# Turning two layers' inputs with VectorE and DRAM instead of TensorE, and a seam listed anew

## The chip, the cores and the metric

One core of a Trainium2 chip runs the whole kernel in one launch, in float32. The metric is the time of one execution on the device in microseconds (us). Four engines compute: TensorE (PE), VectorE (DVE), ScalarE (ACT) and GpSimd (POOL). SyncE (SP) issues nearly all DMA transfers.

## The reference

The input x is (2, 2048, 256): 4096 tokens of 256 features. Four layers follow, each a layer norm, a function and a residual sum:

```python
x = x + attention_a(layernorm(x))   # softmax attention, 16 heads, 4 key heads
x = x + ffn(layernorm(x))           # "rotations", first time
x = x + attention_b(layernorm(x))   # causal linear attention
x = x + ffn(layernorm(x))           # "rotations", second time

def ffn(x):                         # four-layer coupling net, per token: 256-256-128-64-1
    gf = global_net(mean over tokens of x)
    for _ in range(3):
        tf = coupling_net(x)
        x = x + (0.1 + range * (0.7 * gf + 0.3 * tf - 0.5) * 2) * twist(x)

def attention_b(x):                 # 16 heads of 16
    q, k, v = rope(silu(x @ Wq)), rope(silu(x @ Wk)), x @ Wv
    out = tril(q @ k.T) @ v         # no softmax
    out = out * sigmoid(x @ Wg1 @ Wg2)
    return layernorm(out) @ Wo
```

## The kernel before

`xs` holds all tokens in SBUF with tokens on partitions (32 tiles of 128x256); layer norms read it so. Projections need the features on partitions, so each normalised tile must be transposed ("turned"). `zq` is the buffer of all tokens turned, 128 x 2 x 4096, in which the rotations work. The work is cut into eight blocks of 512 tokens (`BLK`), four for each of the two sequences.

`attention_a` runs to about 1500 us, and the first rotations, `rotations(0, ...)`, to about 1690. Then come eight `Block` objects of the linear attention, one loop turn each, to about 1950, and the second rotations, `rotations(1, ...)`, which begin while block 7 is still at work and end at 2102. `in_order(begin)` ties the instructions of PE, DVE, ACT and POOL from line 738 on to the order in which the program lists them; SP's queue keeps its own listed order too. The listing by hand is thus the schedule: an instruction that waits holds up everything that stands behind it on its engine. PSUM gives seven banks in turn (`bank`) and one for the running sums (`ps_state`); a bank's next writer waits for its last reader.

What a turn of the main loop lists, for block x, with y the block after, `after` the one after that, `before` the one ahead:

- `energies(t)`, t = 0 to 3 (L1127, L1133): PE multiplies keys and queries of 128 tokens into four banks, DVE masks them into `en`. `learn(t)` (L1171, L1177) updates the state, `output(t)` (L1144, L1153, L1158) multiplies state and `en` into a bank `bpo`, and DVE gates that into `og`.
- Between them stand y's projections: `query` and `key` (PE L975 pq, pk; ACT silu L1028; POOL products with cosine and sine; DVE shuffles L1035), `rotate` (DVE adds L1047), `narrow` and `gates` (L1069, L1085), `values` (L984 pv), `keys_by_tokens` (PE transposes L996 pt), `halve` and `ready` (ACT L1103 qeo, L1113).
- For the block after that: `look` (DVE statistics of the layer norm, POOL power L111), `norm` (ACT scales into a tile `zt`, L124; POOL adds to xs), and `turn`: `turn(z, bank, evacuate)` makes eight PE transposes of 128x128 into two banks (L131, `bztr`), which ACT copies to `z` (L1022).
- For the finished x: `project_out` (PE L984 pw, L996 pog; DVE statistics L106 to L110 and POOL L111), `add_out` (DVE L1193 into xs). For `before`, whose tokens are then ready for the next layer: `next_look`, `next_norm` (ACT L124 into a tile `zt` of the pool `late`, which has one buffer for it) and `next_turn`: eight PE transposes (L131, `ztr`), which ACT copies to `zq` (L1209) with a sum over the tokens into `sums1`, that the global net needs.

The seam is the change from the first rotations to block 0. `fourth(11, amid)` is the last step of the rotations; for k of 8 and more it is `back`, in which PE transposes blocks of zq back (`turn_back`) and DVE adds them to xs (L879, L912), for two blocks (e) in two halves (h) each. `amid`, called once between the two blocks, lists rotate and key of block 0. After it stand `zero.rotate()` and so on.

The second rotations' tail: when block 7's loop turn is over, its `next_look`, `next_norm` and `next_turn` are listed among `first`, `second`, `third`, `fourth` (PE L817 q1f, L827 q2f, L839 q3f, L852 q4f; ACT a1f, a2f, a3f, cf; DVE and POOL update zq). `context(1)`, resumed by `next(front1)`, is the global net of the second sequence (DVE gmf L781 and L782, PE p1f L786).

Stores to DRAM are already part of `attention_a`: there the key maxima of 128x32 are turned by DVE (L403) and placed through DRAM (dm, L407, L412).

Of the kernel before, what the change touches and what calls it, by code (L numbers as in the profile page):

```python
# [9 lines left out]
F32 = mybir.dt.float32  # L10
F32R = mybir.dt.float32r
AF = mybir.ActivationFunctionType
# [4 lines left out]
P = 128  # L17
B, N, D = 2, 2048, 256
T = B * N
BLK = 512  # L20
NB = T // BLK
# [46 lines left out]
def tile_hybrid(ctx: ExitStack, tc: tile.TileContext, x: bass.AP, consts: bass.AP, wa_d: bass.AP, wf_d: bass.AP, wb_d: bass.AP, out: bass.AP):  # L68
    nc = tc.nc
# [8 lines left out]
    zq = keep.tile([P, 2, T], F32, name="zq")  # L78

    own = ctx.enter_context(tc.tile_pool(name="own", bufs=1))  # L80
    dram = ctx.enter_context(tc.tile_pool(name="a_dram", bufs=2, space=bass.MemoryType.DRAM))
# [12 lines left out]
    def blk(t, j):  # L94
        return t[:, :, j * BLK : (j + 1) * BLK]
# [628 lines left out]
    def behind(tail):  # L724
# [3 lines left out]
        work = ctx.enter_context(tc.tile_pool(name="work", bufs=1, reuse_waits="tile"))  # L728
# [7 lines left out]
        def take(tag, shape, name):  # L736
            if tag == "kt2":
                return work.tile(shape, F32, tag="kt", name=name)
            if tag in ("og", "kt", "swap"):
                return own.tile(shape, F32, tag=tag, name=name, bufs=2 if tag == "swap" else 1)  # L740
            return work.tile(shape, F32, tag=tag, name=name, bufs=rings.get(tag, 1))
# [31 lines left out]
        def rotations(n, part, store):  # L773
# [31 lines left out]
            def blocks(k):  # L805
                return 2 * (k % 4), 2 * (k % 4) + 1
# [59 lines left out]
            def turn_back(k, e, h):  # L866

                j = blocks(k)[e]
                z = blk(zq, j)
                tr = bank(f"trf{n}_{k}_{e}_{h}")  # L870
                for q in range(2):
                    at = slice((2 * h + q) * P, (2 * h + q + 1) * P)
                    for c in range(2):
                        to = q * D + (1 - c) * P
                        nc.tensor.transpose(tr[:, to : to + P], z[:, c, at], ident)
                tr = tr.rearrange("p (q s f) -> p q s f", q=2, s=2)
                half = tokens(j)[:, 2 * h : 2 * h + 2, :].rearrange("p q (s f) -> p q s f", s=2)
                for s in range(2):
                    nc.vector.tensor_tensor(half[:, :, s, :], half[:, :, s, :], tr[:, :, 1 - s, :], ALU.add)  # L879
                return half, tr  # L880
# [5 lines left out]
            def back(k, js, a3, between):  # L886


                q4 = bank(f"q4f{n}_{k}")
                for tile in range(4):  # L890
                    mm(
                        q4[:, 2 * tile : 2 * tile + 2], a3[:, tile * P : (tile + 1) * P], w4_pair,
                        start=True, stop=True,
                    )
                cs = take("small", [P, 3, 8], f"cf{n}_{k}")
                nc.scalar.activation(cs[:, 2, :], q4[:, 0:8], AF.Tanh, bias=hb4, scale=0.5)
                nc.vector.tensor_scalar(cs[:, 0, :], cs[:, 2, :], plain, plains[js[0] // BPB], ALU.mult, ALU.add)
                nc.vector.tensor_scalar(cs[:, 1, :], cs[:, 0, :], -1.0, None, ALU.mult)
                for e in range(2):
                    j = js[e]  # L900
                    if e == 1 and between:
                        between()
                    for h in range(2):
                        half, tr = turned.pop((k, e, h), None) or turn_back(k, e, h)
                        for q in range(2):
                            tile = 2 * h + q

                            x4, t4 = (
                                a.rearrange("p s (u f) -> p (s u) f", u=2) for a in (half[:, q, :, :], tr[:, q, :, :])
                            )  # L910
                            for m, quarters in enumerate((slice(0, 4, 3), slice(1, 3))):
                                nc.vector.scalar_tensor_tensor(  # L912
                                    x4[:, quarters, :], t4[:, quarters, :], cs[:, m, 2 * tile + e : 2 * tile + e + 1],
                                    x4[:, quarters, :], ALU.mult, ALU.add,
                                )
                        if store:
                            s0 = (j % BPB) * BLK + 2 * h * P
                            nc.sync.dma_start(
                                out[j // BPB, s0 : s0 + 2 * P, :].rearrange("(t p) d -> p t d", p=P),
                                tokens(j)[:, 2 * h : 2 * h + 2, :],  # L920
                            )
# [4 lines left out]
        sums1 = hold.tile([P, 2, NB], F32, name="sums1")  # L926
# [72 lines left out]
        class Block:  # L999
# [19 lines left out]
            def turn(self):  # L1019
                j = self.j  # L1020
                self.z = take("z", [P, 2, BLK], f"bz{j}")
                turn(self.zt, lambda c: bank(f"bztr{j}_{c}"), lambda c, tr: nc.scalar.copy(self.z[:, c, :], tr))  # L1022
# [21 lines left out]
            def rotate(self):  # L1044
# [2 lines left out]
                        nc.vector.tensor_tensor(r[:, m, :], r[:, m, :], ts[m], ALU.add)  # L1047
                self.turning = []

            def query(self):  # L1050
                self.q = self.rotated(wq, "qs", "rotq")

# [36 lines left out]

            def keys_by_tokens(self):  # L1090

                self.values(1)
                self.kt = take("kt2" if self.j % 2 else "kt", [P, 4, D], f"kt{self.j}")
                for h in range(2):
                    p = transposed(self.k, h, f"t{self.j}")
                    nc.scalar.copy(self.kt[:, 2 * h : 2 * h + 2, :].rearrange("p t d -> p (t d)"), p)
# [106 lines left out]
                scale(self.fzt, self.tile_of, *self.scales)  # L1203

            def next_turn(self):
                j = self.j
                turn(
                    self.fzt, lambda c: bank(f"ztr1_{j}_{c}"),
                    lambda c, tr: nc.scalar.activation(  # L1209
                        zq[:, c, j * BLK : (j + 1) * BLK], tr, AF.Copy, accum_out=sums1[:, c, j : j + 1]  # L1210
                    ),
                )


        blocks = [Block(j) for j in range(NB)]
# [21 lines left out]
        f = rotations(0, sums0, False)  # L1237
        context, first, second, third, fourth, _ = f
# [72 lines left out]
        zero, one = blocks[0], blocks[1]  # L1311
# [16 lines left out]
            zero.rotate()  # L1328
            zero.key()

        fourth(11, amid)
        zero.rotate()
        zero.narrow()
        zero.values(0)
        zero.gates()
        zero.halve(0)
        zero.keys_by_tokens()
        zero.ready(0)
        one.turn()

        f = rotations(1, sums1, True)
        context, first, second, third, fourth, turn_ahead = f
        front, front1 = context(0), context(1)
        for j, x in enumerate(blocks):
            before = blocks[j - 1] if j else None
            y = blocks[j + 1] if j + 1 < NB else None
            after = blocks[j + 2] if j + 2 < NB else None
            x.energies(0)
            if before:
                before.add_out(1)  # L1350
            if j == NB - 2:
                next(front)
            if y:
                y.query()
            else:
                first(0, 0)
            x.learn(0)
            x.output(0)
            x.energies(1)
            if j == NB - 2:  # L1360
                next(front)
            if before:
                before.next_look()
            if y:
                y.rotate()
                y.key()
            else:
                first(0, 1)
            x.learn(1)
            x.output(1)  # L1370
            if y:
                y.narrow()
            x.energies(2)
            if before:
                before.next_norm()
            if j == NB - 2:
                next(front)
            if y:
                y.gates()
                y.values(0)  # L1380
                y.rotate()
            else:
                first(1, 0)
            if after:
                after.look()
            x.learn(2)
            x.output(2)
            x.energies(3)
            if j == NB - 2:
                next(front)  # L1390
            if y:
                y.keys_by_tokens()
                y.ready(0)
            else:
                first(1, 1)
            if after:
                after.norm(work)
            x.project_out(0)
            x.learn(3)
            x.output(3)  # L1400
            if after:
                after.turn()
            if not y:
                second(0)
            x.add_out(0)
            x.project_out(1)
            if before:
                before.next_turn()
# [6 lines left out]
        fourth(0)  # L1415
        first(2, 1)
        third(1)
        x.next_turn()
        next(front1)
        second(2)  # L1420
# [134 lines left out]
```

## Time and profile before

| | |
|---|---|
| Time, median of 3 runs | 2103.09 us (2100.2 to 2106.34) |
| Profiled execution: its own time | 2103.77 us |
| Profiled execution: span, first to last instruction | 2102.0 us |
| Granted TensorE clock, mean | 0.995 |
| Busy PE, DVE, ACT, POOL | 99%, 81%, 68%, 17% |
| Transposes of PE at L131: bztr, ztr | 64 and 112, of which 64 ztr belong to the second rotations' input |

Times in a profile are those of one execution. An engine's row gives the start, the length, the line and operation, output and inputs, and the idle time before it with what ended it. Matmuls are pipelined, so PE's cost of a step is read from start to start. L12 is line 12 of the kernel before.

### The profile page before, as it was taken

Reading aid. Unit: us, or ns where it says so; the run is one execution under the profiler, and the core shown is the slowest. Engines: PE = TensorE matmul, PEld = TensorE weight load, DVE = VectorE, ACT = ScalarE, POOL = GpSimd, SP = SyncE. Lnnn points to the kernel's source line nnn. Section 1 sums busy time; section 2 is a strip of 40 time slices with the busy share of each in tenths; the row PEclk is TensorE's granted clock in tenths of the full one; section 3 lists DMA queues with packets and bytes.
Section 4 is the critical chain, followed back from the end, with each engine's and each line's share of the span. In section 5 each row is a group of like instructions: output and inputs, shape, how many; then the busy total and the mean of one; then the engine's idle time right before and its main releaser. Section 6 shows DMA issues by size and latency. Waiting matters only on the chain.

```text
span 2102.0 us, 38754 instructions
## 1 busy us (share of the span) xinstructions
PE 2082.3 (99%) x14158; PEld 1010.6 (48%) x14158; DVE 1698.0 (81%) x3241; ACT 1427.3 (68%) x2787; POOL 355.1 (17%) x352
## 2 busy tenths in 40 slices
PE   9999999999999999999999999999999999999998
PEld 4444444444444444444444444444444567776434
DVE  6999988998998999899899899988134678886336
ACT  4477777777777777777777777778864445554443
POOL 3100010000001000000000000000135455542451
PEclk9999999999999999999999999999999999999999
DMA  6511010111101011010110101100100000000002
GB/s 199 149 44 40 18 37 17 50 30 27 38 18 47 10 47 40 17 48 10 47 39 19 38 19 48 37 20 8 53 1 1 0 2 1 1 2 1 1 0 81
DMA packets 59696, 68.72 MB, mean 33 GB/s; under 512 B 24944, under 2 KB 34032, under 8 KB 59248
## 3 DMA queue, kind: packets, MB, share of 16 engines
q1 hardware_dynamic: 58592, 64.79, 11.6%
q8 instruction: 111, 1.82, 0.4%
q10 hardware_dynamic: 720, 0.92, 0.1%
q14 instruction: 81, 0.66, 0.1%
q0 software_dynamic: 192, 0.52, 0.1%
HBM read 35.78 MB, written 26.21 MB: 29 GB/s over the span
## 4 chain that ended last, share of the span: by engine, by line
PE 96%; DVE 2%; DMA 1%; ACT 1%; POOL 0%; issue 0%; SPq 0%; DVEq 0%; ACTq 0%
PE av L632 24%; PE s L376 23%; PE p L650 11%; PE q1f L817 8%; PE p L654 7%; PE q2f L827 4%; PE pe L1127 2%; PE bpo L1153 2%; PE pq L975 1%; PE po L499 1%; PE pw L984 1%; PE pv L984 1%; PE pq L336 1%; PE pk L975 1%; PE q3f L839 1%; PE q4f L852 1%
## 5 line engine op out<-in xcount | busy, mean ns | idle before, releaser
L380 DVE TENSOR_REDUCE mx<-s 128x1 f32<-128x512 f32 x2048 | 1272.8, 682 | 107.0 <-PE s L376 101.2
L658 ACT ACTIVATE e<-p 128x512 f32<-128x512 f32 x2048 | 1057.6, 603 | 308.6 <-PE p L654 301.7
L376 PE MATMUL s<-a_kP,qP 64*128 64x512 f32 x2048 | 706.7, 470 | 4.0 <-DVE mx L380 2.1
L654 PE MATMUL p<-a_m,a_pick 64*128 64x512 f32 x2048 | 580.4, 415 | 0.0
L376 PEld LDWEIGHTS s<-a_kP,qP 64*128 64x128 f32 x2048 | 283.5, 184 | 568.9 <-DVE mx L380 532.1
L632 PE MATMUL av<-e,a_v 128*32 128x512 f32 x4096 | 547.3, 605 | 0.1
L650 PE MATMUL p<-qP,a_kP 64*128 64x512 f32 x2048 | 522.1, 393 | 1.9 <-ACT e L658 1.9
L650 PEld LDWEIGHTS p<-qP,a_kP 64*128 64x128 f32 x2048 | 283.5, 186 | 61.4 <-issue 15.9
L654 PEld LDWEIGHTS p<-a_m,a_pick 64*128 64x128 f32 x2048 | 282.2, 184 | 27.2
L817 PE MATMUL q1f<-zq,wf 128*128 128x512 f32 x384 | 176.1, 601 | 0.0
L632 PEld LDWEIGHTS av<-e,a_v 128*32 128x32 f32 x4096 | 81.0, 108 | 129.1 <-issue 120.0
L398 POOL TENSOR_TENSOR mt<-nm,mt 128x16 f32<-128x16 f32 x31 | 6.9, 222 | 743.9 <-ACT mt L397 743.9
L818 ACT ACTIVATE a1f<-q1f,wf 128x512 f32<-128x512 f32 x96 | 65.8, 686 | 94.5 <-PE q1f L817 91.2
L817 PEld LDWEIGHTS q1f<-zq,wf 128*128 128x128 f32 x384 | 70.3, 190 | 96.9 <-issue 86.2
L1133 DVE TENSOR_TENSOR en<-pe,small 128x512 f32<-128x512 f32 x128 | 79.3, 681 | 14.2 <-PE pe L1127 14.2
L858 DVE TENSOR_SCALAR cf<-cf,f_beta,alphaf 128x512 f32<-128x512 f32 x32 | 32.7, 1022 | 67.7 <-ACT cf L857 67.7
L827 PE MATMUL q2f<-a1f,wf 128*128 128x512 f32 x192 | 87.0, 595 | 0.0
L237 POOL TENSOR_TENSOR ql<-zq,qh 128x512 f32<-128x512 f32 x15 | 19.2, 1283 | 364.2 <-ACT qh L234 364.2
L862 POOL TENSOR_TENSOR tf<-cf,zq 128x512 f32<-128x512 f32 x32 | 56.6, 1768 | 102.4 <-DVE cf L858 101.9
L829 ACT ACTIVATE a2f<-q2f,wf 128x512 f32<-128x512 f32 x48 | 32.6, 685 | 56.2 <-PE q2f L827 56.2
L864 POOL TENSOR_TENSOR zq<-zq,tf 128x512 f32<-128x512 f32 x32 | 56.8, 1775 | 2.5
L491 POOL TENSOR_TENSOR oc<-oc,sums 128x512 f32<-128x512 f32 x16 | 20.5, 1284 | 211.9 <-DMA sums<-dr 140.3
(210 smaller groups left out, 1634.9 us busy)
## 6 DMA issues: line engine op xcount, KB each, us to landing
qP<-dq SPq DMA_DIRECT2D x64, 256.0 KB
dq<-qh SPq DMA_DIRECT2D x62, 128.0 KB
dq<-ql SPq DMA_DIRECT2D x62, 128.0 KB
a_kP<-dk SPq DMA_DIRECT2D x16, 256.0 KB
oc<-avs SPq DMA_DIRECT2D x128, 32.0 KB
sums<-dr SPq DMA_DIRECT2D x128, 32.0 KB
out<-xs SPq DMA_DIRECT2D x16, 256.0 KB
xs<-in_x SPq DMA_DIRECT2D x7, 512.0 KB
```

The costliest lines, as they stand in the source:

```text
L376: mm(s, qP[r // 2][row, qi * P : (qi + 1) * P], kP[r // 2][row, k0 + kb * BLK : k0 + (kb + 1) * BLK], start=True, stop=True,)
L380: nc.vector.tensor_reduce(mx[:, r, qi : qi + 1, kb], s, AX.X, ALU.max)
L632: mm(av[32 * r : 32 * r + 32, :], vA[:, units[u][0] // BPB * KB + kb, 32 * r : 32 * r + 32], es[r], start=(kb == 0), stop=(kb == KB - 1),)
L650: mm(t[r], kP[r // 2][row, k0 : k0 + P], qP[r // 2][row, :], start=True, stop=False)
L654: mm(t[r], pick[row, :], mrow[r // 2][row, :], start=False, stop=True)
L658: nc.scalar.activation(es[r], t[r], AF.Exp, scale=1.0 / HD**0.5)
L817: mm(q1, w1[:, c, m * P : (m + 1) * P], z[:, c, :], start=(c == 0), stop=(c == 1))
L818: nc.scalar.activation(a1[:, m, :], q1, AF.Gelu, bias=b1[:, m : m + 1])
L827: mm(q2, w2[:, c, :], a1[:, c, :], start=(c == 0), stop=(c == 1))
L862: nc.gpsimd.tensor_tensor(t1, cs, z[:, 0, :], ALU.mult)
L864: nc.gpsimd.tensor_tensor(z[:, 1, :], z[:, 1, :], t1, ALU.subtract)
L1133: nc.vector.tensor_tensor(self.ens[t][w], pes[w].rearrange("p (h n) -> p h n", h=4), const("triu").unsqueeze(1).to_broadcast([P, 4, P]), A ...
```

## The change

1. The seam: `back` calls one of two functions before each half of its second block, `amid` before the first half and `zero.rotate` before the second. `zero.values(1)` and `one.turn()` move ahead of `zero.halve(0)` and `zero.keys_by_tokens()`.
2. Blocks 2 to 7 of the linear attention aren't turned by PE. `squares` lets DVE transpose each 128x256 tile of `zt` in place, in squares of 32x32. Four DMAs per tile write the squares to a DRAM tile at the places where they belong, each with 32 partitions x 8 pieces of 32 elements. `fetch` reads the DRAM tile into `z` with two DMAs of 128 x 2 KB. `look` moves up to behind `energies(0)`, `norm` to ahead of `learn(1)`; `squares((0, 1))` stands behind y's `rotate`, `squares((2, 3))` and `fetch` behind y's `ready(0)`. Blocks 0 and 1 are turned by PE as before.
3. `next_turn` does the same for blocks 0 to 6, with a DRAM tile `dz` and two fetches into `zq`; block 7 stays with PE. The sums over tokens come from `next_sum`, two ACT activations from zq to itself with an accumulator, two loop turns later (block 6's ahead of block 7's `next_turn`).
4. `values(1)` is called ahead of `keys_by_tokens` rather than in it, with the same order on PE.

```diff
@@ back
                 for e in range(2):
                     j = js[e]
-                    if e == 1 and between:
-                        between()
                     for h in range(2):
+                        if e == 1 and between:
+                            between[h]()
                         half, tr = turned.pop((k, e, h), None) or turn_back(k, e, h)
@@ Block
+            def squares(self, ts):
+                if 0 in ts:
+                    self.placed = dram.tile([D, BLK], F32, tag="db", name=f"db{self.j}")
+                at = self.placed.rearrange("(b f) (t a i) -> t a f b i", f=32, a=4, i=32)
+                for t in ts:
+                    nc.vector.transpose(self.zt[:, t, :], self.zt[:, t, :])
+                    for a in range(4):
+                        nc.sync.dma_start(
+                            at[t, a], self.zt[32 * a : 32 * a + 32, t, :].rearrange("f (b i) -> f b i", i=32)
+                        )
+
+            def fetch(self):
+                self.z = take("z", [P, 2, BLK], f"bz{self.j}")
+                for c in range(2):
+                    nc.sync.dma_start(self.z[:, c, :], self.placed[c * P : (c + 1) * P, :])
...
             def keys_by_tokens(self):
-                self.values(1)
...
             def next_turn(self):
                 j = self.j
+                if j + 1 < NB:
+                    to = dram.tile([D, BLK], F32, tag="dz", name=f"dz{j}")
+                    at = to.rearrange("(b f) (t a i) -> t a f b i", f=32, a=4, i=32)
+                    for t in range(4):
+                        nc.vector.transpose(self.fzt[:, t, :], self.fzt[:, t, :])
+                        for a in range(4):
+                            nc.sync.dma_start(
+                                at[t, a],
+                                self.fzt[32 * a : 32 * a + 32, t, :].rearrange("f (b i) -> f b i", i=32),
+                            )
+                    for c in range(2):
+                        nc.sync.dma_start(
+                            zq[:, c, j * BLK : (j + 1) * BLK], to[c * P : (c + 1) * P, :]
+                        )
+                    return
                 turn(
...
+            def next_sum(self):
+                for c in range(2):
+                    z = zq[:, c, self.j * BLK : (self.j + 1) * BLK]
+                    nc.scalar.activation(z, z, AF.Copy, accum_out=sums1[:, c, self.j : self.j + 1])
@@ seam
-        fourth(11, amid)
-        zero.rotate()
+        fourth(11, (amid, zero.rotate))
         zero.narrow()
         zero.values(0)
         zero.gates()
+        zero.values(1)
+        one.turn()
         zero.halve(0)
         zero.keys_by_tokens()
         zero.ready(0)
-        one.turn()
@@ main loop
             x.energies(0)
+            if after:
+                after.look()
...
                 y.key()
             else:
                 first(0, 1)
+            if after:
+                after.norm(work)
             x.learn(1)
...
                 before.next_norm()
+            if j > 1:
+                blocks[j - 2].next_sum()
...
             if after:
-                after.look()
+                after.squares((0, 1))
             x.learn(2)
             x.output(2)
             x.energies(3)
...
             if y:
+                y.values(1)
                 y.keys_by_tokens()
                 y.ready(0)
             else:
                 first(1, 1)
             if after:
-                after.norm(work)
+                after.squares((2, 3))
+                after.fetch()
             x.project_out(0)
             x.learn(3)
             x.output(3)
-            if after:
-                after.turn()
...
@@ tail
         third(1)
+        blocks[NB - 2].next_sum()
         x.next_turn()
```

## The prediction

> **What bounds the kernel now.** I read the page first (busy time and chain), then the windows from 1650 us on, then the timelines of PE, DVE and ACT, then the DMA issues.
>
> The page's busy line, and the chain of waits by engine:
>
> ```profile
> PE 2082.3 (99%) x14158; PEld 1010.6 (48%) x14158; DVE 1698.0 (81%) x3241; ACT 1427.3 (68%) x2787; POOL 355.1 (17%) x352
> PE 96%; DVE 2%; DMA 1%; ACT 1%; POOL 0%; issue 0%; SPq 0%; DVEq 0%; ACTq 0%
> ```
>
> PE sets the time. The windows (start:end, length, busy PE, PEld, DVE, ACT, POOL, clock, DMA share) show where it does not:
>
> ```profile
> 1650.00:1700.00 50.00, 47.38 (x219) 27.19 (x216) 39.23 (x126) 25.80 (x48) 18.07 (x21) 1.00 0.00 1
> 1800.00:1850.00 50.00, 50.00 (x531) 38.04 (x530) 43.20 (x117) 27.71 (x62) 28.15 (x31) 1.00 0.01 2
> ```
>
> The first window holds the seam, where PE idles 2.6 us. The second is the linear attention: PE has no gap, but DVE is busy 43.2 of 50, so work moved from PE to DVE has little room. DMA is idle. PE's timeline (start, length, instruction, idle before) at the seam and at two turns:
>
> ```profile
> 1689.38 1.99 PE L984 MATMUL pv<-wb,bz 128*128 128x256 f32 x8
> 1693.72 0.33 PE L996 MATMUL pt<-small,rotk 128*128 128x128 f32 x1 [2.34 <-DVE rotk L1047]
> 1694.32 0.98 PE L996 MATMUL pt<-small,rotk 128*128 128x128 f32 x7 [0.27 <-DVE rotk L1047]
> 1695.14 1.04 PE L131 MATMUL bztr<-small,bzt 128*128 128x128 f32 x8
> 1696.10 1.15 PE L1127 MATMUL pe<-qeo,rotk 32*128 32x256 f32 x16
> ...
> 1753.96 1.09 PE L131 MATMUL bztr<-small,bzt 128*128 128x128 f32 x8
> 1754.89 1.89 PE L984 MATMUL pw<-b_wo,og 128*128 128x256 f32 x8
> ...
> 1757.06 1.04 PE L131 MATMUL ztr<-small,zt 128*128 128x128 f32 x8
> 1758.02 1.24 PE L1127 MATMUL pe<-qeo,rotk 32*128 32x256 f32 x16
> ```
>
> A turn costs PE 0.93 us (bztr, 1753.96 to 1754.89) or 0.96 (ztr, 1757.06 to 1758.02). First energies start at 1696.10, 1726.40, 1758.02, 1789.74, 1821.00, 1852.27, 1883.98 and 1915.86 in the eight blocks: 30.3 for block 0, then about 31.6 each.
>
> **Removed from PE.** Six bztr x 0.93 and seven ztr x 0.96 are 12.3 us, all on the path. That would be the gain if nothing else came late. ACT loses the evacuations and gains next_sum of the same length; it was busy 27.7 of 50 and is covered, except at the tail. Calling values(1) apart from keys_by_tokens leaves PE's order as it was: nothing.
>
> **Added to DVE.** 52 transposes of 128x256. The rows around them:
>
> ```profile
> L403 DVE STREAM_TRANSPOSE mr<-mt x32: 199/201/214, 83.2 to 1464.6; 128x32 f32<-128x32 f32 x32
> ...
> 1771.36 0.72 DVE L1035 STREAM_SHUFFLE swapks<-ks 128x512 f32<-128x512 f32 x1
> 1779.84 0.42 DVE L1177 TENSOR_TENSOR state<-b_sums,small 128x256 f32<-128x256 f32 x1
> 1780.17 0.41 DVE L1158 SCALAR_TENSOR_TENSOR og<-gate,bpo 128x256 f32<-128x256 f32 x1
> ```
>
> An eighth of the width takes 0.20, double the width 0.74; other 128x256 operations start 0.33 apart (1779.84 to 1780.17). I take 0.33 and keep 0.20 and 0.74 as ends. So 2.6 us are added per block of 31.7, where DVE idles about 4.7. What matters is the chain. pv's first half reuses the PSUM bank of the last block's bpo, so it waits for that og, and DVE does this in between, from the end of the last pog: start and BN 1.34, four transposes of next_turn 1.32, en 2.40, look (moved here) 1.85, add_out 0.79, two shuffles 1.26, state and og 0.66, en 2.40, next_look 1.85, rotq add 1.21, two shuffles 1.26, state and og 0.66. The sum is 17.0. PE's own way from there to pv was 16.85 (1757.06 to 1773.91), less ztr 15.89: so PE now waits 1.1 for DVE. From pv to the next ztr it was 14.86 (to 1788.77), less bztr 13.93. New period 17.0 + 13.9 = 30.9, against 31.5 on average in blocks 2 to 5: 0.6 won each, not 1.9. Each 0.1 us per transpose moves a block by 0.4; at 0.74 the blocks 2 to 6 lose 8.2 in all, at 0.20 they win at most the 1.1 each.
>
> **Added to SP, and the new wait of pq.** Each turn is now 16 placements of 256 pieces of 128 bytes and two fetches of 256 KB. Nothing in the trace has the placement's shape. The nearest, stores in 128-byte rows, and the other SP issues of 32 KB:
>
> ```profile
> L407 SPq DMA_DIRECT2D dm<-mr x128: 302/421/1687, 83.4 to 1466.8; - x128
> L479 SPq DMA_DIRECT2D oc<-avs x128: 507/582/1715, 143.0 to 1513.3; - x128
> ...
> 1422.66 1.70 SPq L407 DMA_DIRECT2D dm<-mr  x4
> 1425.49 1.16 SPq L412 DMA_DIRECT2D a_m<-dm  x4
> ```
>
> An issue holds SP 0.42 or 0.58; I take 0.50, with 0.30 and 0.75 as ends. The a_m fetch is issued 1.13 after the last store's issue ends, so 1.55 from its start. qP<-dq, also 256 KB, is read 2.55 to 2.9 after its issue. Per block SP then holds 36 x 0.5 = 18 us of 31, so SP is no bound (its other transfers of this part are the output's, from 2062 on), but its order is: squares((2,3)) issue their last eight after en of tile 3, and the fetch stands behind all sixteen. From PE's last energies: 1.17 to DVE's en, en 2.40, one transpose 0.35, seven issues 3.5, placing 1.55, fetching 2.55: 11.5; the second fetch 0.4 later. PE reached pq 13.17 after those energies (1746.02 to 1759.19), less both turns 11.28. So z comes 0.2 to 0.9 late; I take 0.6. In blocks 2 to 5 that hides in the 1.1 that pv waits anyway. It is paid from block 1 to 2 and may be paid near block 6.
>
> The Trainium skill ("DMA: Bandwidth & Descriptors", Specifications and Anatomy of one DMA) gives at least 512 bytes per piece for line rate, read-modify-write below it, and about 2.0 us fixed per DMA. By that fixed time twice, z would come later by an estimated 0.4 at most, and the pieces of a quarter of that size would not reach full rate; the trace shows 128-byte rows placed within the 1.55 above, for 32 pieces and not 256. The skill's "VectorE: DVE Perf Modes", The three transpose paths, says that DVE transposes only blocks of 32x32, that a 128x128 belongs on TensorE, and that a copy which transposes through strides is 19 times slower than the crossbar's. It speaks against this change; here the strides only move whole rows of 32, so I don't apply the 19.
>
> **Blocks, summed.** Block 0: bztr only, -0.9. Block 1: -1.9 + 0.6 = -1.3. Blocks 2 to 5: 4 x -0.6 = -2.4. Block 6: -0.7. Together -5.3 (ends: -12 with no wait left, +7 with slow transposes or placements).
>
> **Seam.** rotk's add ran after all of fourth(11), ending at 1694.26. Now it stands ahead of the last half; POOL's swapks ends at 1691.45, so the adds end at 1692.7. PE turns bzt in the gap left by pv (1691.4 to 1692.3), then pt to 1693.8. ACT has bv, two copies of bz and qeo, to 1694.0, when energies can start: -2.1 against 1696.10 (ends -1.0 if ACT's copies come in the way, -2.7). DVE's last half moves behind, 1.9 us, and en comes only at 1695.
>
> **Tail.** Block 6's ztr goes, -0.96, but its zt is now read by 16 placements, and there is one such buffer: block 7's scaling waits for them.
>
> ```profile
> 1956.06 2.08 ACT L124 ACTIVATE zt<-xs,nb_f,rs_f 128x256 f32<-128x256 f32 x4 [3.45 <-POOL nb_f L119]
> 1968.27 1.05 DVE L782 TENSOR_SCALAR gmf<-gmf 128x2 f32<-128x2 f32 x1
> ```
>
> From the last pog's end (1949.80): BN 1.4, one transpose, 15 issues 7.5, placing 1.55: 10.8 instead of 6.26, so 4.5 later. Behind it on ACT are a1f, a2f, cf; behind cf, DVE and POOL update zq and gmf, and PE's p1f waits for gmf. gmf ended at 1969.3, so p1f comes at about 1973.7 instead of 1970.06: +3.6 net of the ztr (ends 0, if ACT catches up before p1f, to +7, with issues of 0.75).
>
> **Sum:** -5.3 - 2.1 + 3.6 = -3.8. The profiled execution took 2103.77 (span 2102.0, 1.8 around it), 0.7 above the median of 2103.09. So 2100.0 by it, and 2099.5 for a median.
>
> **Rivals.**
> (1) *Faster*: DVE's chain slips under PE (look and transposes fill idle time, 0.3 each or less), and ACT catches up at the tail. Then nearly all 12.3 + 2.1 go, less some z: -12, 2091. For it: DVE idles 4.7 per block, and PE kept 100%. Against it: the chain of 17.0 has no idle time left in it.
> (2) *Slower*: the SP chain. A placement holds SP 0.70, not 0.50. Then z is late by 0.6 + 8 x 0.2 = 2.2: blocks 2 to 5 pay 1.1 over what they wait anyway, blocks 1 and 6 pay 1.6 each, the tail 16 x 0.2 = 3.2: +10.8 on -3.8 is +7, 2110 to 2111. It decides from about 0.57 per placement, where it eats the 3.8; or from 1 us more in landing. For it: oc's 0.58, single issues up to 1.7, and a placement has a dimension more than any store here. Against: stores of 128-byte rows have 0.42.
> (3) *Nothing measurable*: blocks win less, the seam half. -1, 2102.
>
> **How the numbers follow.** A difference of 0.3%, 6.3 us, is about what a measurement of this kernel can tell from none. Forecast: 0.44, its own range 2093 to 2106 (about a fifth of it beyond -6.3). Rival 1: 0.24. Rival 2: 0.24, reaching with transposes of 0.74 to 2116. Rival 3: 0.08. Faster: 0.24 + 0.10 = 0.34. Slower: 0.24 and 0.02 from the forecast's edge: 0.26. Same: 0.40. The range takes rival 1 to 2089 and rival 2 to 2114.
>
> **What would show it.** Right: no bztr after block 1 but ztr of block 7 alone; PE waits of about 1 us at pv for DVE's og in blocks 2 to 5; energies about 30.9 apart; first energies near 1694; ACT's last zt scaling near 4 us later, behind DMA. PE waiting at pq for DMA by over 1.2 us means rival 2; PE unbroken with periods under 30 means rival 1. A STREAM_TRANSPOSE row far from 0.33 to 0.45, or a placement issue far from 0.50, breaks the sum at that term.

## The result and the profile after

The changed kernel takes 2114.66 us (median of 4) against 2102.51: a ratio of 1.0058, 95% interval 1.0046 to 1.0069. It is slower by 12 us, where 2099.5 was forecast and 2114 was the range's upper end. The profiled execution took 2113.75, its span is 2112.0, so 10.0 longer than before's.

The profile's busy line and its chain of waits, kernel after:

```profile
PE 2076.1 (98%) x14054; PEld 1000.5 (47%) x14054; DVE 1716.9 (81%) x3293; ACT 1420.0 (67%) x2775; POOL 360.8 (17%) x352
PE 93%; DVE 3%; DMA 2%; ACT 1%; POOL 1%; issue 1%; SPq 0%; DVEq 0%; ACTq 0%; POOLq 0%
```

PE does 104 matmuls less and its share of the chain falls from 96% to 93%: it now waits. The windows of the linear attention, the first row before, the others after (columns as in the prediction):

```profile
1750.00:1800.00 50.00, 50.00 (x486) 36.63 (x485) 40.16 (x103) 26.32 (x61) 26.13 (x28) 1.00 0.01 1
1750.00:1800.00 50.00, 44.57 (x430) 30.47 (x430) 40.92 (x116) 17.47 (x40) 24.39 (x26) 0.93 0.34 69
1850.00:1900.00 50.00, 45.01 (x437) 31.02 (x426) 42.19 (x111) 19.14 (x43) 24.28 (x24) 0.97 0.33 68
```

PE had no gap here before. It now idles 5 us of 50, and the clock column says 0.93 and 0.97 where it said 1.00. The waits of PE from 1690 to 1980 us, after (total us, times, longest):

```profile
PE pq L975 <- DMA bz<-db: 11.5, 5, 3.2
PE q1f L817 <- ACT a1f L818: 2.7, 1, 2.7
PE pq L975 <- DVE zt L1229: 1.9, 1, 1.9
PE pgate L1102 <- DVE og L1174: 1.0, 1, 1.0
PE p1f L786 <- DVE gmf L782: 0.6, 1, 0.6
PE pt L996 <- DVE rotk L1047: 0.2, 1, 0.2
...
```

All six blocks turned through DRAM wait at pq, 13.4 us in all. (The third row names DVE's transposes, which ended 0.07 us ahead. pq began 2.63 after the fetch's issue there, and 2.6 to 2.9 after it in the five others, so I count it with them.) Two of these waits on PE's timeline, after:

```profile
1811.75 1.15 PE L1143 MATMUL pe<-qeo,rotk 32*128 32x256 f32 x16
...
1824.62 3.67 PE L975 MATMUL pq<-bz,wb 128*128 128x512 f32 x8 [1.86 <-DVE zt L1229]
...
1857.43 5.30 PE L975 MATMUL pq<-bz,wb 128*128 128x512 f32 x8 [3.21 <-DMA bz<-db]
```

The same eight matmuls take 3.67 us behind a wait of 1.86 and 5.30 behind one of 3.21: the granted clock was halved for 3.4 us there. This happened behind the waits of 2.56, 2.87 and 3.21 in the blocks, some 1.6 to 1.7 us each, and behind the 2.69 in the tail.

First energies of the eight blocks now start at 1691.14, 1722.29, 1753.31, 1787.53, 1821.61, 1853.08, 1887.87 and 1921.31. The difference of the spans splits as follows. The work ahead of the first turn of block 0 ended 2.7 us earlier, in code that the change doesn't touch. (The execution of before had the clock halved for 3.4 us at 27 and again at 314 us, the other didn't; that this is the reason isn't shown.) From that turn to the first energies: 2.3 less (19.7, was 21.9). The seven periods: 230.2, were 219.8, so 10.4 more. Block 7: as before. From its last pog to p1f: 24.5, was 20.3, so 4.3 more. The rest: 0.3 more. The blocks make the loss, and the tail adds to it.

Why z is late shows on DVE and SP. DVE's timeline of one loop turn, after:

```profile
1740.98 2.90 DVE L1047 TENSOR_TENSOR rotk<-rotk,swapks 128x512 f32<-128x512 f32 x2
1743.80 0.76 DVE L1056 STREAM_TRANSPOSE bzt<-bzt 128x256 f32<-128x256 f32 x2
...
1745.13 2.47 DVE L1149 TENSOR_TENSOR en<-pe,small 128x512 f32<-128x512 f32 x4
1747.52 0.74 DVE L1056 STREAM_TRANSPOSE bzt<-bzt 128x256 f32<-128x256 f32 x2
```

And SP's (start, time from the first issue to the end of the last, how many):

```profile
1744.26 8.92 SPq L1058 DMA_DIRECT2D db<-bzt  x16
1754.44 0.82 SPq L1065 DMA_DIRECT2D bz<-db  x2
```

PE's last energies of this turn began at 1743.01. The masks followed 2.1 us later and not 1.17, because the add of rotk had waited for POOL (2.90 for a pair that takes 1.28). The last transpose ended at 1748.26. SP was never idle from the first transpose to the sixteenth issue.

### The profile page after: what moved, and what is told of

Read it like the earlier page. It is cut to its first block, busy times and chain, and to the rows that moved or that the text cites. A ratio compares the mean times of both kernels' runs of the same rounds, so it can differ in the third digit from the quotient of the medians.

```text
span 2112.0 us, 38998 instructions
## 1 busy us (share of the span) xinstructions
PE 2076.1 (98%) x14054; PEld 1000.5 (47%) x14054; DVE 1716.9 (81%) x3293; ACT 1420.0 (67%) x2775; POOL 360.8 (17%) x352
## 4 chain that ended last, share of the span: by engine, by line
PE 93%; DVE 3%; DMA 2%; ACT 1%; POOL 1%; issue 1%; SPq 0%; DVEq 0%; ACTq 0%; POOLq 0%
PE av L632 24%; PE s L376 23%; PE p L650 11%; PE q1f L817 8%; PE p L654 6%; PE q2f L827 4%; PE pv L984 1%; PE pq L975 1%; PE po L499 1%; PE pe L1143 1%; PE bpo L1169 1%; PE pk L975 1%; PE pw L984 1%; PE pq L336 1%; PE q3f L839 1%; DVE mx L380 1%
```

## The experiments

Each kernel is told by its edit to the changed kernel, unless it says otherwise. All ratios are to the kernel before.

**The parts alone.** e1_seam is the kernel before with part 1 of the change, and part 4, which leaves PE's order as it was.

> The kernel before with the first seam listed anew and nothing else. In the changed kernel the first energies came 19.67 us after the first turn of block 0 began, against 21.9 before; if that is the seam's own, this kernel is 2.2 us faster than before, 2101.2 against 2103.4, and PE's wait for rotk falls from 2.6 to 0.2 us. Rival: DVE's last half, now behind rotate, makes the first masks late and PE waits a little later; then no difference.

Measured: 2100.55 us, 0.9988 (0.9979 to 0.9996), and PE's wait at pt:

```profile
PE pt L996 <- DVE rotk L1047: 0.2, 1, 0.2
```

The seam gives 2.9 us by the medians (2103.40 to 2100.55) and 2.5 by the ratio, and PE's wait has fallen from 2.6 us to 0.2 as expected. The next two undo one half of the rest. e2_next turns blocks 2 to 7 on PE as before:

```diff
             x.energies(0)
-            if after:
-                after.look()
...
-            if after:
-                after.norm(work)
             x.learn(1)
...
             if after:
-                after.squares((0, 1))
+                after.look()
...
             if after:
-                after.squares((2, 3))
-                after.fetch()
+                after.norm(work)
...
             x.output(3)
+            if after:
+                after.turn()
```

> The seam and next_turn as in the changed kernel, but blocks 2 to 7 turned by PE as before. Theory S (z comes late because its sixteen placements go out one behind the other on SP): no wait at pq, so six ztr of 0.96 and the seam's 2.2 are won and the tail's 4.3 is lost: about 2099 us against 2102.5. Rival V (VectorE is overloaded by the transposes): PE waits at pv for og all the same, about 2104 to 2107. Both expect the tail's wait of the last scaling for the placements to remain.

Measured: 2100.55 us, 0.9988 (0.9979 to 0.9998), no wait at pq or pv. The periods sum to 215.2 against 219.8, so 4.5 are won in the blocks. Its waits are in the tail:

```profile
PE q1f L817 <- ACT a1f L818: 3.0, 1, 3.0
PE p1f L786 <- DVE gmf L782: 2.2, 1, 2.2
```

Beside e1_seam this is no gain: the tail gives back what the blocks win. e3_blocks keeps the squares and undoes the other half:

```diff
             def next_turn(self):
-                if j + 1 < NB:
-                    ...
                 turn(
...
-            if j > 1:
-                blocks[j - 2].next_sum()
...
-        blocks[NB - 2].next_sum()
         x.next_turn()
```

> The seam and the squares of blocks 2 to 7 as in the changed kernel, but next_turn by PE as before. Theory S: z is as late as in the changed kernel, measured from the first transposes, but PE has its ztr again and reaches pq 0.96 later: waits at pq of about 0.1, 1.6, 1.9, 0.9, 2.2 and 0.8 us instead of 13.4 in all, no halved clock, the tail as before: 2102 to 2104 us. Rival V: VectorE has four transposes less per block, so z comes 1.3 us earlier as well and the waits are gone: about 2095.

Measured: 2108.04 us, 1.0026 (1.0016 to 1.0036). Neither theory's number: the waits at pq are 9.6 us in the profiled execution, the slowest of ten of this kernel (2114.05 us), with the clock halved twice in the blocks. So the squares of blocks 2 to 7 alone cost 7.5 us over the seam (2108.04 to 2100.55), and next_turn's half alone costs nothing. The two together cost 14.1 (2114.66), 6.6 more than one by one. In both kernels the last transpose ends 5.25 us after PE's last energies in most blocks, but PE, without its ztr, is at pq after 11.45 us and not after 12.42. So the 4.5 that next_turn wins in the blocks of e2_next go into waiting, and its tail stays; the other 2 us I can't place.

**What makes z late.** e4_early lists the first squares ahead of the rotate that waits for POOL:

```diff
                 y.values(0)
+            if after:
+                after.squares((0, 1))
+            if y:
                 y.rotate()
             else:
                 first(1, 0)
-            if after:
-                after.squares((0, 1))
```

> The changed kernel with squares((0, 1)) listed ahead of the rotate that waits for POOL, nothing else. Theory S: the first placement goes out 2.8 us earlier, the sixteen end 2.8 us earlier, z too; waits at pq fall from 13.4 to under 1 us, no stretch of halved clock is left but the tail's, PE now waits about 1 us per block at pv for og: about 2101 us. Rival D (what makes z late is the landing of the last eight placements and the fetch, behind the second pair of transposes, which stay where they are): z is as late as now, 2114 us.

Measured: 2108.37 us, 1.0025 (1.0015 to 1.0035). Half of what theory S forecast. The waits at pq fell only to 8.2 us, though the first issue went out 2.8 us earlier relative to PE's energies in most blocks. SP then stood idle for up to 2.1 us in the middle of the sixteen. The last transpose moved up by 0 to 0.7 us, 0.5 on average, and z by 0.9. e6_quad packs the placements:

```diff
-                at = self.placed.rearrange("(b f) (t a i) -> t a f b i", f=32, a=4, i=32)
+                at = self.placed.rearrange("(b f) (t a i) -> a f t b i", f=32, a=4, i=32)
                 for t in ts:
                     nc.vector.transpose(self.zt[:, t, :], self.zt[:, t, :])
-                    for a in range(4):
-                        nc.sync.dma_start(
-                            at[t, a], self.zt[32 * a : 32 * a + 32, t, :].rearrange("f (b i) -> f b i", i=32)
-                        )
+                for a in range(4 if 3 in ts else 0):
+                    nc.sync.dma_start(
+                        at[a], self.zt[32 * a : 32 * a + 32, :, :].rearrange("f t (b i) -> f t b i", i=32)
+                    )
```

(next_turn likewise. SP is added to the engines of `in_order`, here and in e8 to e12.)

> The changed kernel with four placements per turn instead of sixteen: one DMA for each 32 partitions takes all four tiles, issued after the fourth transpose; the pieces of 128 bytes, their number and places, and all lists of the other engines stay. SP keeps the order of the program. Theory S (the number of issues on SP makes z late): placements end 1.5 to 2 us after the last transpose, z comes 4 to 6 us earlier, no waits at pq, no halved clock in the blocks; PE waits about 1 us per block at pv for og; the last scaling waits no more: about 2094 to 2097 us. Rival D (writing 4096 pieces of 128 bytes makes z late): the landing grows from 1.3 to about 6 us, waits at pq stay as in the changed kernel, 2110 to 2115 us.

Measured: 2113.92 us, 1.0053 (1.0040 to 1.0065): nothing is won in total. SP's timeline of e6_quad:

```profile
1750.04 2.77 SPq L1058 DMA_DIRECT2D db<-bzt  x4
1756.66 0.80 SPq L1065 DMA_DIRECT2D bz<-db  x2
```

Twelve issues fewer, yet the fetch came 5.0 to 6.9 us after the last transpose, where sixteen placements had 5.0 to 6.2. The four start only after the last transpose, hold SP 0.68 each, and their last pieces land 1.5 to 3 us after the last issue, against 0.85 us in most groups before. That fewer issues won nothing and earlier first issues only half gave theory T: z comes about 7.7 us after the last transpose whatever the packing, so what counts is where that transpose stands. e9_all_early moves all four:

```diff
                 y.values(0)
+            if after:
+                after.squares((0, 1, 2, 3))
+            if y:
                 y.rotate()
             else:
                 first(1, 0)
-            if after:
-                after.squares((0, 1))
...
-                after.squares((2, 3))
                 after.fetch()
```

> The changed kernel with all four squares of a block ahead of the rotate that waits for POOL, still sixteen placements, fetch where it was, SP in program order. Theory T (z comes about 7.7 us after the last transpose however the placements are packed, so it is the place of that transpose on VectorE that makes it late): the last transpose ends about 6 us earlier, sixteen issues take 7.9, landing 1.3, fetch 2.4, so z is there 0.5 us ahead of PE; with an issue of 1.2 to 1.7 us in most groups some waits of up to 1 us stay, 13.4 us of waits fall to about 4, no halved clock is left but the tail's: 2100 to 2104 us. Rival V (VectorE has too much to do): the masks come later, PE waits at pv for og instead, 2108 or more.

Measured: 2104.05 us, 1.0004 (0.9995 to 1.0013). The last transpose now ends 0.2 us before PE's last energies and not 5.25 after; the waits at pq fall from 13.4 to 2.6 us and the clock stays whole in the blocks. PE now waits 4.9 us for og, 3.9 of it at pv, where it waited 1.0 in all. Here the sixteen issues do count: from this earlier transpose the fetch takes 8 to 9.7 us. e10_early_quad joins this with e6_quad's packing, and frees the tail:

```diff
             def next_norm(self):
-                self.fzt = late.tile([P, 4, D], F32, tag="zt", name=f"zt1_{self.j}")
+                self.fzt = (late if self.j + 1 < NB else work).tile([P, 4, D], F32, tag="zt", name=f"zt1_{self.j}")
```

> As e9_all_early with four placements of all tiles per turn instead of sixteen, and block 7's zt for the second rotations in the buffer that the linear attention's zt leaves free, so that its scaling needn't wait for block 6's placements. Theory T: z is there 4 us ahead of PE, which covers slow issues and landings; no waits at pq; up to 1 us per block at pv for og; the tail as before: 2090 to 2096 us. Rival D: the landing of 4096 small pieces takes over 6 us and waits at pq stay, over 2100 us.

Measured: 2098.22 us, 0.9976 (0.9967 to 0.9985), 2 us above the upper expectation. No wait at pq is left. PE's waits in e10_early_quad:

```profile
PE pv L984 <- DVE og L1174: 4.9, 4, 1.3
PE pgate L1102 <- DVE og L1174: 1.2, 2, 1.0
PE p1f L786 <- DVE gmf L782: 0.7, 1, 0.7
```

This is DVE's chain from the prediction, seen by itself: 1.1 to 1.3 us per block at pv, in four blocks.

**That chain.** e12_look_early is e10_early_quad with look one loop turn earlier, where DVE waits for pog:

```diff
         one.norm(late)
+        blocks[2].look()
...
             x.energies(0)
-            if after:
-                after.look()
...
+            if j + 3 < NB:
+                blocks[j + 3].look()
             x.project_out(0)
```

> As e10_early_quad (2098.2 us, PE waiting 4.9 us for og at pv in four blocks and 1.2 at pgate), with look of each block one loop turn earlier, where VectorE waits for pog (block 2's ahead of the seam). Theory V2 (what is left is VectorE's chain of 17.0 us from pog to the og that frees pv's bank, in which look takes 1.85): the chain is shorter than PE's own way of 15.9, the waits for og are gone, periods fall from 31.1 to about 29.9: 2092 us. Rival: the chain is set by POOL or ScalarE, or look is as much in the way at its new place (pog's statistics then come later), 2096 to 2098 us.

Measured: 2091.76 us, 0.9940 (0.9927 to 0.9954), the fastest of all, and close to the 2091 that rival 1 had for the change as it stood. Periods are 29.5 to 29.9 for blocks 0 to 5. PE's waits in e12_look_early from 1685 to 1985 us, all of them:

```profile
PE p1f L786 <- DVE gmf L782: 0.7, 1, 0.7
PE pt L996 <- DVE rotk L1047: 0.4, 2, 0.2
PE pgate L1102 <- DVE og L1174: 0.2, 1, 0.2
```

**The tail.** e8_next_quad is e2_next with e6_quad's packing, and e11_next_tail adds e10_early_quad's line for `next_norm`:

```diff
-                    at = to.rearrange("(b f) (t a i) -> t a f b i", f=32, a=4, i=32)
+                    at = to.rearrange("(b f) (u t a i) -> u a f t b i", f=32, t=4, a=4, i=32)
...
```

> As e2_next (seam and next_turn through DRAM, blocks turned by PE as before), with four placements per turn instead of sixteen. e2_next measured 2100.55 us with PE waiting 3.0 us for a1f and 2.2 for gmf in the tail. Theory S: the last scaling starts 5 us earlier, both waits go, and so does the stretch of halved clock: 2100.5 - 5 - 1.7 = about 2094 us. Rival D: the landing of the bigger placements takes the place of the issues, 2099 to 2101 us.

> As e8_next_quad (2099.05 us), with block 7's zt for the second rotations in its own buffer as in e10_early_quad. If the 2.2 us at p1f and the halved clock behind them come from the scaling that waits for block 6's placements, both go: 2099 - 2.2 - 1.7 = about 2095 us. If p1f waits for the sums of block 6 (next_sum behind its fetch), the wait stays and the time is 2098 to 2099 us.

Measured: 2099.05 (0.9978, 0.9969 to 0.9987) and 2095.90 (0.9965, 0.9952 to 0.9978). The packing took away the wait at q1f, but the last scaling still began 8.4 us after the last pog; p1f kept its 2.2 us and a halved clock. With a buffer of its own the wait at p1f is 0.7 and the clock stays whole. So the tail's loss was the one buffer of zt, with the placements reading it.

**The clock.** e5_filler gives PE idle work ahead of pq:

```diff
                 p = bank(f"p{name}_{m}")
+                for i in range(fill if m == 0 else 0):
+                    nc.tensor.transpose(p[:, i % 4 * P : (i % 4 + 1) * P], ident, ident)
...
```

(`fill` is 8 for the queries of blocks 2 to 7 and else 0.)

> The changed kernel with eight idle PE transposes of the identity (0.93 us) put ahead of pq in blocks 2 to 7; they write into pq's bank, which pq then overwrites. If PE idling for over 2.3 us is what halves its clock for 3.41 us, the waits shrink to 0.1 to 2.3 us, no halving is left there and the time falls by 3 x 1.7 = 5 us to about 2109.5 although PE does more. If the halved clock has another cause, or costs nothing, the time stays at 2114.7 or rises by up to 1.

Measured: 2114.71 us, 1.0056 (1.0041 to 1.0071), no change. Halved stretches in the blocks fell from three to one, but the waits only from 13.4 to 9.2 for some 6 of filler: a slow issue (1.97 us) left a wait of 3.1 and a late landing one of 2.5. The wait at p1f grew from 0.6 to 2.2 as well. The time thus neither bears out nor refutes the price of the clock. The periods lean to it: they sum to 229.2, 1.0 less than in the changed kernel, where 6 of filler less 4.2 of waits would make them 2 longer and two stretches of 1.65 less take off 3.3. Otherwise the price rests on the rows of pq.

## Why the prediction was wrong

**The step that failed** is the time of z: "From PE's last energies: 1.17 to DVE's en, en 2.40, one transpose 0.35", then 7.6 for issues, placing and fetching, against PE at pq after 11.28. The second part held: blocks 5 and 7, with no slow issue, needed 7.61 (1817.00 to 1824.62) and 7.96 from the last transpose to pq. PE's 11.28 was 11.0 to 11.45. The first part did not: the last transpose ended 5.25 after the energies in most blocks and not 3.92. I took 1.17 from a place where DVE waits for PE; here DVE was a microsecond behind, on the rotk add that waits for POOL and two transposes of squares((0,1)), and of squares((2,3)) I had counted one transpose. That is 1.3 of lateness in most blocks (0.4 in block 2, 1.8 in block 6).

**Slow transfers had a row but no term.** One issue in 33 held SP for 1.2 to 1.8 us (7 of 234), which with 16 placements per turn met about every second group. In the four blocks with such an issue the way from the last transpose to pq was 8.2 to 9.1 us, in three of them over 8.7. I had named such issues for the rival and left them out of the forecast's 0.6. So z was late by 1.1 to 3.2, 2.2 on average.

**The halved clock had no term at all.** The Trainium skill ("TensorE: Matmul & The Clock Gate", Part 1: The HAM clock gate) says that PE falls to half rate after at least one idle window of about 3.4 us. Here PE never idled 3.4 us in the blocks, and waits of 2.56 and more still halved the clock for 3.4 us; those of 1.9 and less did not in this execution. Three times 1.65 is 5.0 us.

**What became of the sum.** e12_look_early, with the same parts and nothing late in the blocks, has periods that sum to 209.8; the changed kernel's sum to 230.2. Of these 20.4 us, 13.4 are pq's waits, 1.0 pgate's, 5.0 the clock; 1.0 I can't place. The forecast had 214.5 (5.3 won): 4 to 5 for DVE's chain at pv and half a microsecond for z. The chain was right: e10_early_quad shows it and e12_look_early removes it. But in the changed kernel it never shows, because z's lateness hides it. I had put the cover the other way round.

**Terms that held.** Seam -2.1: 2.3 in the trace, 2.9 in e1_seam. Tail +3.6: 4.3; the last scaling began 11.1 after the last pog (10.8 forecast), behind DMA as named. That the size held is partly luck: I had all of the loss come at p1f, but PE waited 2.7 at q1f for a1f, lost some 1.7 to the halved clock behind that, and waited 0.6 at p1f. A transpose 0.33: 0.34 apart, 0.40 long. An issue 0.50: 0.49 apart. (The 2.0 us per DMA in the Trainium skill, "DMA: Bandwidth & Descriptors", Anatomy of one DMA, is a fit for DMAs that GpSimd issues; here SP issues them, and the two terms of the sum, 1.55 for placing and 2.55 for fetching, measured 1.7 to 1.9 and 2.6 to 2.9.) ACT's scaling row, after:

```profile
1966.37 2.07 ACT L124 ACTIVATE zt<-xs,nb_f,rs_f 128x256 f32<-128x256 f32 x4 [9.27 <-DMA dz<-zt]
```

**The rival** that won, slower by z, had the right place and decision point (over 1.2 us late at pq, which its test named), and 2110 to 2111. Its mechanism was wrong: placements cost 0.50 and not 0.70. Its price also lacked the clock, whose 5.0 us are more than the 4 by which it fell short.

## What to carry to other kernels

Work taken off the bounding engine pays only where its result returns in time: a detour through DRAM has a length of its own (7.6 to 9.1 us from the last transpose in the changed kernel), so ask first where its last producer stands in its own engine's order, and take that from the row of that very stage, not from one where the engine was idle. Moving the producer up, then packing the transfers and giving the tail its own buffer, then shortening the next chain turned a loss of 12 us into a gain of 12 to 13.

Price the neighbours too: a buffer that a DMA reads is not free when its last compute reader has gone, and a stall of a PE that was never idle can cost more than its length.

## What the runs showed of the hardware

A halved clock came behind single waits of PE of 1.84 to 3.4 us, and not each time: the seam's 2.34 before and waits of up to 3.04 in the experiments passed without. It lasted 3.4 us, three times 6.8. Where the waits lie seems to decide. In each profiled run all halved stretches begin on one grid of 3.413 us: in the changed kernel, 1792.45, 1857.30 and 1969.94 come 10, 29 and 62 steps after 1758.31. Between 1640 and 2050 us of all these runs, a step at full clock in which PE idled 1.97 us or more was followed by a halved one each time (12 of 12), one in which it idled 1.55 or less never, and of seven with 1.65 to 1.84 four were. So 1.84 us within one step were enough in e3_blocks, while 3.04 across two steps, 1.84 and 1.20, passed in e2_next. No run varied this alone. The two steps in e3_blocks (columns as in the windows above; the clock is the third number from the end):

```profile
1859.66:1863.07 3.41, 1.57 (x8) 0.69 (x5) 3.30 (x7) 0.97 (x3) 0.14 (x1) 1.00 0.50 154
1863.07:1866.48 3.41, 3.41 (x6) 1.33 (x5) 2.44 (x12) 0.60 (x1) 2.27 (x3) 0.50 0.00 0
```

A DMA of 1024 pieces of 128 bytes holds SP 0.68 us and one of 256 pieces 0.45, half as much again for four times the pieces, while 4096 pieces in four DMAs land some 4.2 us after the first issue at best. VectorE transposes 128x256 float32 in place in 0.40 us, as long as its other operations of that shape:

```profile
L1229 DVE STREAM_TRANSPOSE zt<-zt x28: 401/403/446, 1754.5 to 1957.8; 128x256 f32<-128x256 f32 x28
```
